# Three score blocks of a slice in one run, and a new timetable, in a graph-attention layer on one Trainium2 core

## The chip, the core and the metric

The kernel runs on one core of a Trainium2 chip. A core has TensorE (PE, matrix products, with the loading of its weights shown as PEld), VectorE (DVE), ScalarE (ACT), GpSimd (POOL) and SyncE (SP), each with its own instruction stream, and DMA queues that move data between the chip's main memory and the on-chip memory SBUF. PE writes to PSUM, a small memory that DVE and ACT read. The metric is device time in microseconds of one execution, as the median of several runs.

## What is computed

128 graphs of 128 nodes and 768 features, 12 heads of 64, everything in 32-bit floats. In short:

```python
h = maximum(layernorm(x), 0)
q, k, v = split_heads(h @ Wq + bq), split_heads(h @ Wk + bk), split_heads(h @ Wv + bv)
s = einsum('bhqd,bhkd->bhqk', q, k) / sqrt(64) + beta * adj
s = where(adj > 0, s, -9e15)
out = x + merge_heads(einsum('bhqk,bhkd->bhqd', softmax(s), v))
```

## The kernel before

**Groups and slices.** Four graphs make a group (G, 32 of them). For each group the projections come in three slices: `qk0` (Q and K of heads 0 to 5), `v`, and `qk1` (Q and K of heads 6 to 11). A slice is a product of 512 rows by 768 by 768. From group 1 on it is made in the manner of fast matrix multiplication: the 2x3 blocks of activations and 3x3 blocks of weights are combined so that 15 products (`PRODUCTS`) replace the 18 of the plain way, and each of them again takes 7 zones in place of 8. Group 0 goes the plain way (`plain_slice`), while the combined weights (T tiles, 448 KB each) are made and stored in main memory.

**A product** (L681, in `product`) is 7 zones of two 64-column halves, 28 instructions in the trace. Products with the same chain letter (a to d) add up in the same PSUM pair; after each, `evict` takes the running sum out into the home of each block of the result in which it is used. The first that a home receives opens it: before, for Q and K, three ACT operations (640 columns at L724, then twice 128 with the bias at L726); for V, DVE adds the bias to 256 columns (L711) and ACT copies the other 640 (L716). All later ones are DVE accumulations of 896 columns (L704). There are 4 PSUM pairs; a chain's next product has to wait until the evictions of the one before it have read the pair. When a block is complete, `decode` adds its zones (four POOL operations at L739 to L742 for Q and K, five at L750 to L754 for V); DECODE says when, and for a few blocks that DVE does it ("v").

**Attention.** A block `oc` (0 to 5) is a pair of heads for the group's four graphs. `scores` (L776, 32 instructions on 64x64 quarters) writes to a PSUM pair, `mask` (L789, DVE) adds the bias and frees the pair, `expo` (L798, ACT) takes the exponential, `attend` (L855, 32 instructions) multiplies by V, `drain` (ACT), `recip` (DVE), `divide` (eight ACT operations), `add` (DVE, L904) and `send` (SP) finish it. An attend is a generator: `turn()` emits 4 of its instructions after each zone of the products that follow. The three blocks of `qk0` are scored while the V slice runs, those of `qk1` while the next group's `qk0` runs. `to_hT` (L580, DVE) turns the activations of the next group, `inner` (POOL) and ten `sum_acts` (L585, DVE) combine them.

**The order** of every engine's stream is written out: `put(at, f)` puts an action on a heap of due times, and after each product `slice_z` runs what is due. A group is 45 slots long, one for each product: `qk0` has slots 0 to 14, `v` 15 to 29, `qk1` 30 to 44, and a time past 45 lies in the next group. TABLE has the due times of a group, FIRST, SECOND and LAST exceptions for the first and last groups, EVICT and DECODE the offsets of evictions and decodes from their product, ORDER the order of the products in a slice. Group 0's slices go by another mechanism (`then(n, f)`: lists of actions for each product, and `later`, `trailing`, `masking`).

**Transfers.** 10 of the 45 T tiles stay in SBUF (RESIDENT gives their positions in the sequence of 45). The others come through a ring of 6 buffers; `load_T` issues the next load (SP) right behind the product that frees a buffer.

## Time and profile before

| | |
|---|---|
| median of 3 runs | 2667.59 us (2667.44 to 2669.44) |
| span of the profiled execution | 2664.1 us |
| mean granted clock of PE | 0.998 |
| first product of group 1 begins at | 122.1 us |
| DMA: moved, mean rate | 736.65 MB, 277 GB/s |

The span goes from the first to the last instruction of the profiled execution; a time of that execution by the clock of the runs isn't given, and the median of the runs is 3.5 us longer than the span. The page gives each engine's busy time, the chain of work that ended last, and the costliest groups of instructions (line, engine, operation, output and inputs, count, busy time and mean ns of one, idle time before them and what ended it). The timeline merges like instructions and gives start, duration and count; a duration of merged PE rows reaches to the end of the last instruction, which overlaps with the next row.

### The profile page before, as it was taken

To read this page: it belongs to the slowest core of one execution; us is meant where nothing else is said; L and a number is where in the kernel's file an instruction comes from. 1 tells how busy PE (TensorE), PEld (TensorE's weight loads), DVE (VectorE), ACT (ScalarE), POOL (GpSimd) and SP (SyncE) were. 2 spreads that over 40 slices of the span, in tenths; PEclk is the share of its full clock that TensorE was granted. 3 is DMA by queue.
4 is the path that set the end of the run, shared out by engine and by line. 5 is a ranking of instruction groups with operands and counts; after the bars stand their busy time and mean duration, and the time that the engine had idled before them with its cause. 6 is when DMAs were issued, how large, how long until landed. Compare 5 with 4: busy or idle time off the path is not lost.

```text
span 2664.1 us, 121442 instructions
## 1 busy us (share of the span) xinstructions
PE 2644.1 (99%) x52041; PEld 2564.2 (96%) x52041; DVE 2165.8 (81%) x2702; ACT 1755.1 (66%) x4608; POOL 2097.8 (79%) x3043
## 2 busy tenths in 40 slices
PE   9999999999999999999999999999999999999998
PEld 8799999999999999999999999999999999999997
DVE  7878887878888788887788887888877888778876
ACT  2567766677666677666777666776667776667654
POOL 5877778877779777788777797777887777887774
PEclk9999999999999999999999999999999999999999
DMA  8899999998989999999999899999899898999885
GB/s 254 276 281 279 282 284 278 283 292 267 293 281 279 287 277 284 281 281 280 289 269 288 281 281 282 288 275 285 279 278 292 268 291 279 276 286 282 256 253 165
DMA packets 531572, 736.65 MB, mean 277 GB/s; under 512 B 106444, under 2 KB 371160, under 8 KB 531032
## 3 DMA queue, kind: packets, MB, share of 16 engines
q1 hardware_dynamic: 530384, 728.06, 88.5%
q8 instruction: 411, 6.73, 1.0%
q14 instruction: 129, 1.06, 0.1%
q10 hardware_dynamic: 648, 0.79, 0.1%
HBM read 662.22 MB, written 66.51 MB: 274 GB/s over the span
## 4 chain that ended last, share of the span: by engine, by line
PE 94%; DVE 1%; DMA 0%; issue 0%; ACT 0%; SPq 0%; DVEq 0%; ACTq 0%
PE pair L681 80%; PE pair L776 7%; PE pair L855 6%; PE pair L1048 1%; DVE home L704 0%; DMA x<-in_x_dram 0%; DMA T_qk<-kept_qk 0%; PE pair L926 0%; DVE e L789 0%; DVE prep_qk L403 0%; ACT e L836 0%; DVE res_qk L403 0%; PE pair L947 0%; DVE e L931 0%; ACT e L933 0%
## 5 line engine op out<-in xcount | busy, mean ns | idle before, releaser
L704 DVE TENSOR_TENSOR home<-home,pair 128x896 f32<-128x896 f32 x836 | 880.0, 1077 | 220.5 <-PE pair L681 179.8
L681 PE MATMUL pair<-sbig,T_qk 128*64 128x128 f32 x13020 | 827.6, 274 | 2.3 <-DVE home L704 1.2
L681 PEld LDWEIGHTS pair<-sbig,T_qk 128*64 128x64 f32 x13020 | 702.5, 137 | 19.9 <-issue 12.1
L739 POOL TENSOR_TENSOR home<-home 128x256 f32<-128x256 f32 x308 | 266.1, 864 | 320.0 <-DVE home L704 319.7
L681 PE MATMUL pair<-T_v,sbig 128*64 128x128 f32 x7812 | 457.8, 273 | 1.6 <-ACT home L716 0.6
L681 PE MATMUL pair<-A,T_qk 128*64 128x128 f32 x6944 | 445.6, 273 | 0.9 <-issue 0.9
L681 PEld LDWEIGHTS pair<-T_v,sbig 128*64 128x64 f32 x7812 | 430.7, 137 | 8.4 <-ACT e L836 4.8
L855 PE MATMUL pair<-v,e 128*64 128x65 f32 x6048 | 403.5, 221 | 0.0
L836 ACT ACTIVATE e<-e,sm 128x64 f32<-128x64 f32 x1512 | 381.7, 341 | 7.4 <-DVE sm L824 6.1
L681 PEld LDWEIGHTS pair<-A,T_qk 128*64 128x64 f32 x6944 | 384.6, 137 | 1.5 <-issue 1.5
L855 PEld LDWEIGHTS pair<-v,e 128*64 128x64 f32 x6048 | 362.2, 137 | 3.2
L724 ACT ACTIVATE home<-pair 128x640 f32<-128x640 f32 x340 | 240.6, 708 | 188.5 <-PE pair L681 187.2
L681 PE MATMUL pair<-sbig,res_qk 128*64 128x128 f32 x4340 | 312.3, 273 | 0.4
L742 POOL TENSOR_TENSOR home<-home 128x256 f32<-128x256 f32 x308 | 269.7, 876 | 24.1
L885 ACT ACTIVATE sm<-pair,tiny 128x8 f32<-128x8 f32 x189 | 50.8, 269 | 329.5 <-PE pair L855 329.5
L789 DVE SCALAR_TENSOR_TENSOR e<-pair,biasT 128x1024 f32<-128x1024 f32 x189 | 229.4, 1214 | 34.1 <-PE pair L776 33.0
L740 POOL TENSOR_TENSOR home<-home 128x256 f32<-128x256 f32 x308 | 228.2, 741 | 24.1
L681 PEld LDWEIGHTS pair<-sbig,res_qk 128*64 128x64 f32 x4340 | 238.0, 137 | 1.4 <-DVE home L704 1.3
L560 ACT ACTIVATE x<-x,block 128x192 f32<-128x192 f32 x480 | 222.6, 540 | 0.0
L726 ACT ACTIVATE home<-pair,bqk 128x128 f32<-128x128 f32 x680 | 214.3, 377 | 0.0
L798 ACT ACTIVATE e<-e 128x1024 f32<-128x1024 f32 x189 | 196.1, 1055 | 21.8 <-DVE e L789 14.0
L741 POOL TENSOR_TENSOR home<-home 128x128 f32<-128x128 f32 x308 | 175.6, 570 | 24.2
(208 smaller groups left out, 4401.6 us busy)
## 6 DMA issues: line engine op xcount, KB each, us to landing
T_qk<-kept_qk SPq DMA_DIRECT2D x713, 448.0 KB
T_v<-kept_v SPq DMA_DIRECT2D x372, 448.0 KB
xo<-in_x_dram SPq DMA_DIRECT2D x190, 256.0 KB
out_dram<-xo SPq DMA_DIRECT2D x189, 256.0 KB
x<-in_x_dram SPq DMA_DIRECT2D x248, 192.0 KB
sbig<-in_x_dram SPq DMA_DIRECT2D x116, 384.0 KB
kept_qk<-prep_qk SPq DMA_DIRECT2D x23, 448.0 KB
adj<-in_adj_dram SPq DMA_DIRECT2D x128, 64.0 KB
```

The lines of the kernel that those rows point to most:

```text
L560: nc.scalar.activation(t, t, AF.Relu, bias=shift[G, n], scale=rstd[G, n])
L681: nc.tensor.matmul(p[q:q + HD, at, :], lhs[:, q:q + HD], rhs, start=(first and at % 4 == 0), stop=True, skip_group_check=True)
L704: nc.vector.tensor_tensor(t, t, p[:, 0:7], op)
L724: nc.scalar.activation(t[:, 0:5], p[:, 0:5], AF.Copy, scale=float(sign))
L726: nc.scalar.activation(t[:, at], p[:, at], AF.Identity, bias=bqk[:, of, oc:oc + 1], scale=float(sign))
L739: e.tensor_tensor(t[:, 1:4:2], t[:, 1:4:2], twice(5), ALU.add)
L740: e.tensor_tensor(t[:, 2:5:2], t[:, 2:5:2], twice(1), ALU.add)
L742: e.tensor_tensor(t[:, 0:7:6], t[:, 0:7:6], twice(2), ALU.add)
L789: nc.vector.scalar_tensor_tensor(e[:, :, at], ps[:, :, at], SCORE_CAP * ISCALE, bias[:, :, at], op0=ALU.min, op1=ALU.add)
L798: nc.scalar.activation(e, e, AF.Exp, scale=1.0 / ISCALE)
L836: nc.scalar.activation(o[:, r, b, 0:HD], pa[:, r, b, 0:HD], AF.Copy, scale=t[:, 1, r, b:b + 1])
L855: nc.tensor.matmul(pa[q:q + HD, 2 * g + i, :], k[:, q:q + HD], vt[G, "v", r, h // 4][:, 4 * g + h % 4, :], start=True, stop=True, skip_gro ...
```

## The change

- **Score runs.** In TABLE, the three `scores` entries of each Q/K slice get due times that fall in one slot, with no other PE work due between them (before: two in one slot, the third some slots later). The blocks of a run come in another sequence (1, 0, 2 and 0, 2, 1 of the slice's three).
- **Product orders.** One ORDER for all groups (the last group's `qk1` keeps its own); the first slice begins 4, 1, 8, 5, which completes chain d before the scores.
- **Openings.** OPEN, empty before, names products whose opening goes another way: 2 is all on DVE, 1 splits off the last 384 columns (Q, K) to DVE. With the new orders and offsets, 2 takes effect in a middle group for two openings of `qk0` (both uses of product 4) and three of `v` (both of product 4, and product 5). `bqk` grows to 8 columns, the first five zero, so that one DVE operation adds the bias to 896 columns.
- **Attends.** Blocks in WHOLE (2, 3, 5) are emitted in one piece.
- **Decodes.** All new offsets. In a middle group DVE decodes V block (1, 1) and Q/K block (0, 2) of `qk1`; before, only block (0, 0) of `qk1`.
- **Timetable.** TABLE, EVICT, DECODE and LAST anew, EARLY for group 0's actions in place of its lists, OVER for single entries of the first groups. RESIDENT names other positions.
- `needs` and `did` only check the order while the program is built; they issue nothing.

```diff
-ORDER = {"qk0": (1, 0, 5, 2, 10, 3, 6, 7, 13, 11, 9, 4, 14, 12, 8), "v": (1, 0, 5, 2, 10, 3, 6, 7, 13, 11, 4, 9, 14, 8, 12), "qk1": (4, 1, 0, 8, 2, 5, 3, 6, 7, 10, 9, 13, 11, 12, 14)}
+ORDER = {'qk0': (4, 1, 8, 5, 0, 3, 2, 10, 7, 6, 11, 9, 13, 14, 12), 'v': (4, 1, 8, 5, 3, 10, 0, 7, 2, 13, 6, 11, 9, 14, 12), 'qk1': (4, 0, 3, 8, 2, 1, 7, 6, 5, 9, 11, 10, 12, 14, 13)}
-RESIDENT = (10, 12, 16, 21, 29, 33, 36, 39, 41, 42)
+RESIDENT = (0, 5, 14, 16, 22, 24, 27, 31, 38, 39)
 TABLE = (
...
-    (5.399, 'sum', 'S5'), (8.41, 'sum', 'S14'), (9.857, 'sum', 'S11'), (17.129, 'scores', 0, 2),
-    (17.594, 'mask', 2), (18.011, 'exp', 2), (17.884, 'scores', 0, 1), (20.163, 'mask', 1),
-    (23.187, 'exp', 1), (23.44, 'scores', 0, 0), (24.691, 'mask', 0), (26.808, 'xo', 2),
...
-    (47.396, 'scores', 1, 2), (47.912, 'mask', 5), (47.949, 'scores', 1, 0), (49.895, 'add', 0),
-    (49.151, 'mask', 3), (51.424, 'send', 0), (50.757, 'exp', 5), (51.214, 'scores', 1, 1),
...
+    (8.583782, 'sum', 'S11'), (9.005184, 'sum', 'S5'), (9.963287, 'sum', 'S14'), (18.715354, 'scores', 0, 1),
+    (18.71757, 'mask', 1), (18.718354, 'scores', 0, 0), (18.721354, 'scores', 0, 2), (19.858615, 'mask', 2),
+    (19.938663, 'exp', 2), (26.447577, 'exp', 1), (27.850478, 'mask', 0), (35.49811, 'xo', 2),
...
+    (45.127516, 'attend', 0), (45.60572, 'divide', 1), (48.381413, 'drain', 0), (48.750402, 'add', 1),
+    (48.785602, 'recip', 0), (48.985172, 'scores', 1, 0), (48.988172, 'scores', 1, 2), (48.991022, 'mask', 3),
+    (48.991172, 'scores', 1, 1), (49.260051, 'mask', 5), (51.074388, 'divide', 0), (51.320856, 'send', 1),
...
+    (0, 'drain', 4): 61.5908, (2, 'norm', 3, 2, 4): 66.1614, (2, 'sum', 'S1'): 81.7354, (0, 'drain', 5): 60.3658,
...
+    (0, 'exp', 4): 58.1173, (1, 'xo', 3): 102.7651, (0, 'scores', 1, 0): 48.8393, (0, 'recip', 3): 56.1085,
...
+WHOLE = (2, 3, 5)
 OPEN = {
+    ('qk0', 0): 2, ('qk0', 3): 2, ('qk0', 4): 2, ('qk0', 7): 1, ('qk0', 8): 2, ('qk0', 10): 2,
+    ('qk0', 11): 1, ('qk0', 12): 2, ('qk0', 13): 1, ('qk1', 8): 2, ('qk1', 9): 1, ('qk1', 10): 1,
+    ('qk1', 11): 2, ('qk1', 13): 1, ('v', 0): 1, ('v', 4): 2, ('v', 5): 2, ('v', 6): 2,
+    ('v', 7): 1, ('v', 9): 2, ('v', 12): 1,
 }
...
                 bias = bv_b[:, j * 2 * P:(j + 1) * 2 * P].rearrange("p (i n) -> p i n", i=2)
                 nc.vector.tensor_tensor(t[:, 5:7], bias, p[:, 5:7], op)
-                if split:
+                if split == 2:
+                    nc.vector.tensor_scalar(t[:, 0:5], p[:, 0:5], float(sign), None, op0=ALU.mult)
+                elif split:
...
-                if split:
+                if split == 2:
+                    nc.vector.tensor_tensor(t, bqk[:, 0:7, oc:oc + 1].to_broadcast([P, 7, P]), p[:, 0:7], op)
+                elif split:
...
     def attend(G, oc, behind=None):
-        between.append(attend_steps(G, oc, behind))
+        steps = attend_steps(G, oc, behind)
+        if (G or oc > 2) and oc in WHOLE:
+            for _ in steps:
+                pass
+        else:
+            between.append(steps)
...
+    def run_until(at):
+        while events and events[0][0] < at:
+            _, _, f, args = heapq.heappop(events)
+            f(*args)
...
     for G in range(NG):
...
+        for n, (at, name, *args) in enumerate(TABLE):
+            if placed(G, at, name, args):
+                put(OVER.get((G - NG if G == NG - 1 else G, name, *args), max(45 * G + at, 45 + 0.001 * n)), actions[name], G, *args)
```

The exceptions in OVER that concern scores are: group 0, `scores` 1, 2 at 46.7153 and 1, 0 at 48.8393; group 1, 0, 0 at 63.8665, 1, 0 at 93.9684 and 1, 1 at 94.5242; group 2, 0, 0 at 108.7881 and 0, 2 at 108.7766.

## The prediction

> **What bounds the kernel now.** I read the page's busy table and its chain that ended last first, then TensorE's (PE's) waits, then its timeline.

> ```profile
> span 2664.1 us, 121442 instructions
> ...
> PE 2644.1 (99%) x52041; PEld 2564.2 (96%) x52041; DVE 2165.8 (81%) x2702; ACT 1755.1 (66%) x4608; POOL 2097.8 (79%) x3043
> ...
> PE 94%; DVE 1%; DMA 0%; issue 0%; ACT 0%; SPq 0%; DVEq 0%; ACTq 0%
> PE pair L681 80%; PE pair L776 7%; PE pair L855 6%; PE pair L1048 1%; DVE home L704 0%; DMA x<-in_x_dram 0%; DMA T_qk<-kept_qk 0%; PE pair L926 0%; DVE e L789 0%; DVE prep_qk L403 0%; ACT e L836 0%; DVE res_qk L403 0%; PE pair L947 0%; DVE e L931 0%; ACT e L933 0%
> ```

> The end is set by PE: 94% of the chain is PE following PE. L681 are the products, L776 the scores, L855 the attends. The waits of PE say how little another engine holds it up:

> ```profile
> PE pair L1369 <- DVE over L970: 3.6, 1, 3.6
> PE pair L681 <- issue: 2.4, 6, 1.1
> PE pair L681 <- DVE home L704: 2.2, 2, 1.2
> ```

> Columns: total us, times, longest. In 2664 us the products wait 2.2 us for an eviction. So an edit on DVE, ACT or POOL can gain almost nothing here, only lose; a gain must come out of PE's own stream. There, one group repeats; the chain in order of time has the same piece at

> ```profile
> 919.46 4.80 PE pair L681 x88
> ...
> 1000.51 4.80 PE pair L681 x88
> ```

> that is, every 81.05 us. One slice of such a group, on PE:

> ```profile
> 1048.19 1.70 PE L681 MATMUL pair<-res_v,sbig 128*64 128x128 f32 x28
> 1049.72 1.70 PE L681 MATMUL pair<-T_v,sbig 128*64 128x128 f32 x28
> 1051.34 1.98 PE L776 MATMUL pair<-home 64*64 64x128 f32 x64
> 1053.25 4.81 PE L681 MATMUL pair<-T_v,sbig 128*64 128x128 f32 x84
> 1057.89 1.70 PE L681 MATMUL pair<-res_v,A 128*64 128x128 f32 x28
> 1059.41 3.23 PE L681 MATMUL pair<-T_v,sbig 128*64 128x128 f32 x56
> 1062.57 1.10 PE L776 MATMUL pair<-home 64*64 64x128 f32 x32
> 1063.61 3.28 PE L681 MATMUL pair<-T_v,A 128*64 128x128 f32 x56
> 1066.71 3.23 PE L681 MATMUL pair<-T_v,sbig 128*64 128x128 f32 x56
> ```

> Columns: start, duration, instructions; only differences of starts count, since durations overlap. A product (28 instructions) takes 1049.72 - 1048.19 = 1.53 us. From 1049.72 to 1057.89 lie four products and two score blocks (x64): 8.17 - 6.12 = 2.05 us for the two. From 1059.41 to 1066.71 lie four products and one block (x32): 7.30 - 6.12 = 1.18 us. So a further block in a run costs 2.05 - 1.18 = **0.87 us**, and a run costs **0.31 us** beside its blocks, whatever its length. The shapes show where it lies: the scores use 64x64 quarters of the array, the products 128x64 halves, and PE loses time on the way in (1051.34 is 0.09 after 1049.72 + 1.53) and out.

> ```profile
> 1004.93 0.39 PE L681 MATMUL pair<-sbig,T_qk 128*64 128x128 f32 x4
> 1005.15 0.40 PE L855 MATMUL pair<-v,e 128*64 128x65 f32 x8
> ...
> 1007.39 1.70 PE L681 MATMUL pair<-sbig,res_qk 128*64 128x128 f32 x28
> ```

> An attend is woven into one product; that product takes 2.46 us, so the attend 0.93. Check: 45 x 1.53 + 6 x 0.93 + 2 x (2.05 + 1.18) = 80.9 of the 81.05. The group is accounted for by PE alone.

> **The change, part by part.** *Score runs.* Before: each of the 61 Q/K slices scored in groups 1 to 31 (31 first ones, 30 second ones; the last is cut in halves) has a run of two and one of one, 122 runs; group 0 adds 6: 128. After: one run of three a slice, where the three entries fall in one slot with no other PE work between them (18.715 to 18.721 and 48.985 to 48.991, slot 18 and slot 3). Exceptions are read from OVER: group 0's second slice has two runs (46.7; 48.8 and 48.99), group 1's second two (93.97 and 93.99; 94.52). That gives 3 + 2 + 1 + 2 + 30 + 29 = 67. 61 runs go: 61 x 0.31 = **19.0 us less**. A run of three isn't in the trace; I take 1.18 + 2 x 0.87 = 2.92, the step from one to two repeated. Bounds: nothing, if a third block were as dear as a run of its own (1.18), and these 19.0: 0.87 is 32 instructions at half of a product's pace (1.53 / 28 = 0.0546), two at once, and a block has no reason to go below that.

> *Attends whole.* WHOLE emits blocks 2, 3 and 5 (93 in all) in one piece instead of woven in. The end of the kernel has such a piece:

> ```profile
> 2644.17 1.10 PE L947 MATMUL pair<-v,e 128*64 128x65 f32 x32
> 2645.10 0.39 PE L681 MATMUL pair<-sbig,T_qk 128*64 128x128 f32 x4
> ```

> 32 instructions of the same shape in 0.93 us: as much as woven. I take 0. [...]

> *Openings, decodes, DVE.* OPEN moves two Q/K openings from ACT to DVE in the first slice (one 128x896 operation each, instead of three on ACT) and the 640-column part of three V openings; one V decode goes from POOL to DVE. ACT (66%) and POOL (79%) only gain. The rows for DVE:

> ```profile
> L704 DVE TENSOR_TENSOR home<-home,pair 128x896 f32<-128x896 f32 x836 | 880.0, 1077 | 220.5 <-PE pair L681 179.8 <-POOL A L590 36.7 <-ACT sbig L521 2.1
> L789 DVE SCALAR_TENSOR_TENSOR e<-pair,biasT 128x1024 f32<-128x1024 f32 x189 | 229.4, 1214 | 34.1 <-PE pair L776 33.0
> L904 DVE TENSOR_TENSOR xo<-xo,e 128x512 f32<-128x512 f32 x186 | 161.8, 870 | 0.1
> L580 DVE STREAM_TRANSPOSE A<-x 128x512 f32<-128x512 f32 x186 | 129.2, 696 | 0.1
> L585 DVE TENSOR_TENSOR sbig<-sbig,A 128x896 f32<-128x896 f32 x93 | 118.5, 1274 | 1.0
> ...
> L742 DVE TENSOR_TENSOR home<-home 128x256 f32<-128x256 f32 x32 | 28.3, 883 | 1.1
> L740 DVE TENSOR_TENSOR home<-home 128x256 f32<-128x256 f32 x32 | 26.4, 825 | 1.1
> ...
> L741 DVE TENSOR_TENSOR home<-home 128x128 f32<-128x128 f32 x32 | 21.8, 681 | 1.1
> L739 DVE TENSOR_TENSOR home<-home 128x256 f32<-128x256 f32 x32 | 20.6, 644 | 0.0
> ```

> Operations overlap by some 0.08 us: four back to back take 4.08, not 4 x 1.08:

> ```profile
> 1067.00 4.08 DVE L704 TENSOR_TENSOR home<-home,pair 128x896 f32<-128x896 f32 x4 [0.51 <-PE pair L681]
> ```

> Added for a group: 2 x 1.0, 3 x 0.75 (5/7 of a row of L704, which also reads PSUM), and a V decode, five operations of 128 or 256 columns like those of L739 to L742: nothing to 3.8, I take 3.0. That is 7.2 us on an engine with 81% of 81 us, so near 90%. The first slice is the full one. By the new due times it holds, on DVE, 11 accumulations and 2 openings (13.0), 3 masks (3 x 1.13), 5 activation sums (5 x 1.19), a Q/K decode (2.7), 2 adds (1.6) and 3 turns (1.9): **28.5 us**, against PE's 15 x 1.53 + 2 x 0.93 + 2.92 = **27.7**. Before, that slice had

> ```profile
> 1000.50:1029.50 29.00, 29.00 (x590) 28.42 (x586) 25.10 (x28) 19.64 (x60) 25.85 (x31) 1.00 0.89 277
> ```

> (PE, PEld, DVE, ACT, POOL busy): DVE 25.1 of 29.0. The overflow of 0.8 us runs into the V slice, where DVE has some 21 us of work in 27.7. So it needn't stop PE, but the places are tight. Product 8 follows product 4 on the same PSUM pair after one product only and must wait for both evictions of 4, 2.1 us on DVE; the attend due in slot 45.1 lies woven into that product (1.53 + 0.93 = 2.46), which leaves 0.4 us for both hand-overs. The product behind a run of three takes the pair that the first mask frees: the mask has two blocks, 1.74 us, for its 1.21. Bounds: 0, and the whole overflow, 0.8 us a group. I take 0.1 a group (a fourth of one such margin), 30 x 0.1 = **3 us more**.

> *Product orders, residents, DMAs.* The work stays: 45 products a group at 1.53, ten tiles kept, so 35 loads of 448 KB a group as before. The longest stretch of the sequence without a kept tile falls from 12 products (positions 43 to 9) to 8 (6 to 13). SP's issues (inputs, sends, loads of T) are the same in number; each T load still stands behind its product, whose pace sets it. 0.

> *Start and end.* Group 0's actions get due times of their own, group 1 other offsets, the last group's V slice another order. The two wait rows of L681 (2.4 + 2.2) hold what can go; bounds -4.6 and, as much again added, +4.6. Group 1's first slice has one of the two DVE waits (1.2) and a new order: I take **-1**.

> Sum for the profiled execution: span 2664.1 - 19.0 + 3.0 - 1.0 = 2647.1. The median, 2667.6, lies 3.5 above the span; I take that as unchanged: **2650.6 us**.

> **The rivals.** *DVE becomes the bound in the first slice.* For it: 28.5 against 27.7. Against: the V slice gives it back, and PSUM holds four pairs. Price: 0.8 x 30 = 24 instead of 3: 2671.6 if all of it stops PE, 2659.6 if half; within 0.2% for the most part.

> *POOL's decodes come late for three blocks at once* (the slower side). A run of two needed four of six decoded tiles; the run of three needs all six, and the last block had five more slots before.

> ```profile
> L739 POOL TENSOR_TENSOR home<-home 128x256 f32<-128x256 f32 x308 | 266.1, 864 | 320.0 <-DVE home L704 319.7
> ...
> L742 POOL TENSOR_TENSOR home<-home 128x256 f32<-128x256 f32 x308 | 269.7, 876 | 24.1
> ...
> L740 POOL TENSOR_TENSOR home<-home 128x256 f32<-128x256 f32 x308 | 228.2, 741 | 24.1
> ...
> L741 POOL TENSOR_TENSOR home<-home 128x128 f32<-128x128 f32 x308 | 175.6, 570 | 24.2
> ```

> One decode is 3.05 us on POOL. For the V slice's run, four stand in a row behind the eviction of product 9: 12.2 us. On PE, from the end of product 9 to the third block lie products 13, 14, 12, then 4, 1, 8, 5 (7 x 1.53), two attends (1.86) and two blocks (1.83): 14.4. Less about 1.1 for that eviction, some 1 us remains. If DVE's lag eats this and one operation more (0.75), PE waits 0.75 in each of 61 runs: 46 us, 2696. It decides from 0.31 a run.

> *Whole attends wait for weights.* At a load per 54.6 ns, the product's own pace (1.53 / 28), 32 take 1.75: 0.82 x 93 = 76 us, 2727. The row of L947 speaks against. [...]

> *The runs aren't joined* (PE work slips between): 2669.6, the sum without the 19. Against: the due times.

> **How the numbers follow.** My forecast, 2644 to 2660: 0.74. A larger gain, all waits of the start gone (below 2644): 0.03. DVE's bound: 0.12, a quarter of it still faster. Runs not joined: 0.02. POOL's decodes: 0.08. Whole attends: 0.01. The range 2643 to 2666 leaves out POOL, the attends, the unjoined runs, about half of DVE's case and part of the larger gain, 0.19. 0.2% is 5.3 us, about what a measurement of this kernel can tell from no change: faster 0.74 + 0.03 + 0.03 = 0.80, within 0.11, slower 0.09.

> **What would show it.** In the changed profile: score rows of x96 on PE, 2.92 us of cost by the same difference of starts; the period of a group at 80.4; attends of x32 in 0.93; DVE near 90%; PE's waits for L704 small. Rows "scores <- POOL home" would show the POOL rival, products waiting for DVE by whole microseconds a group the DVE one. I am wrong if the period stays at 81 or above.

## The result, and the profile after

| | before | after |
|---|---|---|
| median | 2668.52 us (4 runs, 2667.44 to 2670.2) | 2770.25 us (4 runs, 2758.72 to 2776.61) |
| span of the profiled execution | 2664.1 us | 2767.5 us |
| mean granted clock of PE | 0.998 | 0.996 |
| first product of group 1 | 122.1 us | 123.3 us |

The ratio is 1.0374 (95% interval 1.0349 to 1.0398): 102 us slower, where 17 us faster was forecast. In the changed kernel the products are at L796, the scores at L901, the attends at L990. The page of the changed kernel, its busy table and its chain:

```profile
span 2767.5 us, 121305 instructions
...
PE 2657.5 (96%) x52041; PEld 2584.2 (93%) x52041; DVE 2344.5 (85%) x3018; ACT 1640.2 (59%) x4327; POOL 1901.2 (69%) x2883
...
q1 hardware_dynamic: 529856, 727.80, 90.8%
q8 instruction: 411, 6.73, 1.0%
...
PE 92%; issue 4%; DMA 2%; DVE 2%; SPq 0%; ACT 0%; POOL 0%; ACTq 0%; DVEq 0%; POOLq 0%
```

PE has the same 52041 matmuls, and the chain still runs on PE, but 4% of it is now "issue", which was 0%: time in which an engine waits for nothing that the profile shows. PE's waits in the changed kernel (total us, times, longest):

```profile
PE pair L796 <- issue: 47.3, 41, 3.1
PE pair L901 <- issue: 32.1, 30, 3.1
PE pair L990 <- issue: 7.8, 10, 1.7
PE pair L1494 <- DVE over L1107: 3.6, 1, 3.6
PE pair L559 <- DVE st L547: 2.4, 1, 2.4
PE pair L796 <- DMA T_v<-kept_v: 2.4, 1, 2.4
```

Over all rows of this view, PE's waits for other engines and for data sum to 17.7 us, against 13.1 before. Its waits for "issue" went from 2.6 us (7 times) to 87.2 us (81 times). The windows view of the same stretch in both kernels (us, then busy us and instructions of PE, PEld, DVE, ACT, POOL, then clock, DMA share, GB/s), first before:

```profile
300.00:2600.00 2300.00, 2297.42 (x46566) 2249.61 (x46564) 1879.96 (x2234) 1561.80 (x4102) 1848.13 (x2653) 1.00 0.91 280
```

and after:

```profile
300.00:2600.00 2300.00, 2215.83 (x44632) 2175.63 (x44628) 1963.13 (x2417) 1410.17 (x3717) 1595.24 (x2408) 1.00 0.94 270
```

PE stood 2.6 us there before and 84.2 us after, and got through 4% fewer matmuls.

**What "issue" is here.** The timeline of PE in the changed kernel, around one stop:

```profile
672.35 1.70 PE L796 MATMUL pair<-T_v,A 128*64 128x128 f32 x28
673.88 1.70 PE L796 MATMUL pair<-T_v,sbig 128*64 128x128 f32 x28
675.50 2.88 PE L901 MATMUL pair<-home 64*64 64x128 f32 x96
678.31 2.84 PE L796 MATMUL pair<-T_v,sbig 128*64 128x128 f32 x48
683.60 2.19 PE L796 MATMUL pair<-T_v,sbig 128*64 128x128 f32 x36 [2.45 <-issue]
```

PE stops in the middle of a product, after 20 of its 28 instructions, where it can wait for no tile. The row "q8 instruction" above has 411 packets of 16 KB, and from the start of one to the start of the next PE began 256.1 instructions in the mean, in either kernel (matmuls and weight loads counted together, with the few others of PE). The stop lies, by the count below, at one and the same place of every 256; I call it a block boundary. The DMA view of 681.0 to 682.2 us has one of them:

```profile
q1 hardware_dynamic: 94, 0.30, 85.7%
q8 instruction: 1, 0.02, 5.6%
```

and the same view from 676 to 681 has none, only data, 103.9% of the time of the engines by this view:

```profile
q1 hardware_dynamic: 716, 1.34, 103.9%
```

By the trace's record this packet, from here on a **refill**, ran from 681.08 to 682.16, and PE went on at 683.60. I numbered PE's instructions and looked at every gap: 101 lie at the same place, within three instructions of 194 past a multiple of 256, and sum to **107.4 us** above the usual pitch. Before: 10 such gaps, 3.1 us. (The sum depends on the usual pitch that is taken off: with the median step from one matmul's start to the next, the same 101 gaps give 115.0 us, and the 10 before 3.9.) All other gaps went from 15.3 to 20.2 us. So the span comes apart as 2664.1 - 19.0 (score runs, below) + 104.3 (these stops) + 4.9 (other gaps) + 5.3 (an estimate: 0.2% for the mean granted clock, 0.996 where it was 0.998) = 2759.6, against 2767.5; 8 us I could not place, about what the choice of the pitch makes.

A refill can be followed in three pieces: from PE passing the instruction 165 past a multiple of 256 (a fixed mark of mine; between 300 and 2500 us each refill of both kernels began 12 instructions behind it or later) to its start, the **wait**; its own duration, 1.06 us before and 1.12 after; and from its end to PE going on, 1.47 us at the stops (middle eight tenths 1.33 to 1.64). From the mark to the place of the stops behind the next multiple of 256 (193 past it) lie 284 instructions. How long PE takes for them is the **cover**: a slice with dense short instructions has a short one (5.5 us at slot 3 of the changed kernel, 7.7 at slot 24). PE stopped where wait + 1.1 + 1.5 was more than the cover: between 300 and 2500 us this sum, taken refill by refill, names all 83 of the gaps over 0.3 us at this place in the changed kernel and all 7 in the one before, and 20 and 8 refills more, late by 0.33 and 0.22 us at most. Means by the slot in which PE passes the mark, in us, and the stops that followed between 300 and 2500 us, worked out from the trace:

| slot | wait before | cover before | wait after | cover after | stops after |
|---|---|---|---|---|---|
| 3 | 2.6 | 6.9 | 2.8 | 5.5 | 0.8 |
| 6 (after: 5) | 3.8 | 6.3 | 3.1 | 7.3 | 0.0 |
| 15, 16 | 3.5, 3.7 | 6.2, 6.3 | 4.6, 4.7 | 6.3, 6.2 | 27.0 |
| 18 | 2.6 | 7.6 | 5.5 | 6.1 | 29.4 |
| 24, 25 | 2.0, 1.2 | 7.6 | 2.2, 1.7 | 7.7 | 0.0 |
| 37, 41 | 1.7, 1.8 | 6.7, 7.1 | 4.6, 5.8 | 6.8, 7.3 | 23.9 |

Two things changed: the waits grew (mean 2.47 to 3.49 us, longest 5.0 to 7.3), most at slots 15 to 18 and 37 to 1; and where scores lie closer together the cover shrank, since score instructions passed in about half the time (96 in 2.88 us, against 28 in 1.53). Put through the same rule one refill after the other, the changed kernel's waits and covers give 101 us; its covers with waits of before, drawn slot by slot, 9 us; its waits with covers of before 80 us. So, by this working, the refills' lateness is the larger part, and before there was hardly any room: at slot 6, 3.8 + 1.1 + 1.5 is 6.4 for a cover of 6.3.

### The profile page after: what moved, and what is told of

Same layout as the page of the kernel before. It is cut to its first block, busy times and chain, and to the rows that moved or that the text cites. A ratio compares the mean times of both kernels' runs of the same rounds, so it can differ in the third digit from the quotient of the medians.

```text
span 2767.5 us, 121305 instructions
## 1 busy us (share of the span) xinstructions
PE 2657.5 (96%) x52041; PEld 2584.2 (93%) x52041; DVE 2344.5 (85%) x3018; ACT 1640.2 (59%) x4327; POOL 1901.2 (69%) x2883
## 4 chain that ended last, share of the span: by engine, by line
PE 92%; issue 4%; DMA 2%; DVE 2%; SPq 0%; ACT 0%; POOL 0%; ACTq 0%; DVEq 0%; POOLq 0%
PE pair L796 76%; PE pair L901 6%; PE pair L990 6%; PE pair L1185 3%; DMA xo<-in_x_dram 1%; DVE home L820 1%; DMA sbig<-in_L_gnn_Wk_dram 0%; PE pair L1403 0%; DMA sbig<-in_x_dram 0%; DMA out_dram<-xo 0%; PE pair L1190 0%; DVE sbig L690 0%; SPq L412 0%; DMA T_v<-kept_v 0%; DVE e L915 0%
## 5 line engine op out<-in xcount | busy, mean ns | idle before, releaser
L796 PE MATMUL pair<-sbig,T_qk 128*64 128x128 f32 x13888 | 866.9, 273 | 9.2 <-issue 7.2
L796 PEld LDWEIGHTS pair<-sbig,T_qk 128*64 128x64 f32 x13888 | 782.2, 137 | 15.8 <-issue 12.8
L796 PE MATMUL pair<-A,T_qk 128*64 128x128 f32 x6944 | 427.0, 273 | 2.5 <-DVE sbig L839 1.6
L796 PEld LDWEIGHTS pair<-A,T_qk 128*64 128x64 f32 x6944 | 386.6, 137 | 3.9 <-issue 1.9
L796 PE MATMUL pair<-T_v,sbig 128*64 128x128 f32 x5208 | 320.1, 276 | 33.3 <-issue 30.5
L796 PEld LDWEIGHTS pair<-T_v,sbig 128*64 128x64 f32 x5208 | 294.6, 138 | 43.0 <-issue 41.1
L990 PE MATMUL pair<-v,e 128*64 128x65 f32 x6048 | 323.4, 221 | 8.7 <-issue 7.8
L990 PEld LDWEIGHTS pair<-v,e 128*64 128x64 f32 x6048 | 300.1, 137 | 16.1 <-issue 12.0
L796 PE MATMUL pair<-T_v,A 128*64 128x128 f32 x4340 | 260.4, 273 | 0.1
L796 PE MATMUL pair<-res_v,sbig 128*64 128x128 f32 x3472 | 239.4, 273 | 1.7 <-issue 1.7
L796 PEld LDWEIGHTS pair<-T_v,A 128*64 128x64 f32 x4340 | 239.3, 137 | 1.5 <-ACT home L835 0.4
L655 ACT ACTIVATE x<-x,block 128x192 f32<-128x192 f32 x480 | 226.1, 540 | 6.4 <-DMA T_v<-kept_v 3.6
L901 PE MATMUL pair<-home 64*64 64x128 f32 x5312 | 182.9, 274 | 26.4 <-issue 26.3
L796 PE MATMUL pair<-sbig,res_qk 128*64 128x128 f32 x3472 | 207.3, 273 | 0.5 <-issue 0.5
```

Of the source, the lines that this page charges most:

```text
L655: nc.scalar.activation(t, t, AF.Relu, bias=shift[G, n], scale=rstd[G, n])
L796: nc.tensor.matmul(p[q:q + HD, at, :], lhs[:, q:q + HD], rhs, start=(first and at % 4 == 0), stop=True, skip_group_check=True)
L901: nc.tensor.matmul(ps[k:k + HD, i, g * N:(g + 1) * N], keys[r, k:k + HD], queries[r], start=True, stop=True)
L990: nc.tensor.matmul(pa[q:q + HD, 2 * g + i, :], k[:, q:q + HD], vt[G, "v", r, h // 4][:, 4 * g + h % 4, :], start=True, stop=True, skip_gro ...
```

## The experiments

The theories: **data**, refills come late because of the data transfers' timetable (RESIDENT, input loads, SP's order); **density**, PE's instructions lie too densely (runs of three, whole attends), whatever the data do. In the texts that were on record ahead of the runs, the letters change: up to e7_light_before and in e11_split1, A is both together, B the data alone and C density alone; in e8_x_times, e9_resident, e12_all_dma and e13_res2, B is the data, with B1 for the input loads and B2 for the T loads; in e4_before_whole and from e14_res3 on, A is the data. In e17_x_late a "trigger" is PE passing the mark. Runs without a ratio beside them are single executions, and the four of the changed kernel lie up to 18 us apart; so they are read by their stops first.

**Density.** e1_woven and e3_split and e5_woven_split change the changed kernel; e11_split1 too; e4_before_whole changes the kernel before.

```diff
-WHOLE = (2, 3, 5)                      # e1, e5 (drains 4 and 5 a slot later)
+WHOLE = ()
-(18.721354, 'scores', 0, 2)            # e3, e5 (with its mask and exp)
+(20.72, 'scores', 0, 2)
-(48.991172, 'scores', 1, 1)
+(51.2, 'scores', 1, 1)
-(18.721354, 'scores', 0, 2)            # e11
+(19.75, 'scores', 0, 2)
-(48.991172, 'scores', 1, 1)
+(49.9, 'scores', 1, 1)
```

> The changed kernel with WHOLE = (): all attends woven into products again, the drains of blocks 4 and 5 one slot later so that they stand behind their attends. Score runs stay joined. Theory A (PE's instruction blocks of 256 arrive late because the joined score runs and whole attends use them up too fast AND because the refill stands behind data transfers): some of the 107 us of stops at block boundaries goes, time 2700 to 2745 us. Rival B (only the backlog of data transfers of the new timetable makes the refill late; how dense PE's instructions are doesn't matter): 2760 to 2775, as the changed kernel. Rival C (only density matters): like A here.

2780.8 us, stops 95.3 us: the time didn't fall and the stops did by 12 us only, so whole attends don't make most of the loss.

> The changed kernel with the third score block of each run taken two slots later (18.72 to 20.72 and 48.99 to 51.2, groups 1 and 2 partly as they were), so runs of two and one again; attends stay whole. About 57 runs more: +18 us in every theory. A: the stops in slots 18 to 21 (70 of 107 us) fall by half or more, sum 2720 to 2755. B: nothing but the runs, 2780 to 2795. C: as A or lower.

2826.3 us, stops 85.4, but other gaps 78.4. The two largest of PE's waits are

```profile
PE pair L797 <- DVE e L916: 37.6, 28, 1.3
PE pair L902 <- issue: 37.1, 32, 2.7
```

The first is a wait for a mask that this edit itself makes late. The stops fell by 22 us, where theory A asked for 35 at slots 18 to 21 alone; the time, outside every forecast because of that mask, says nothing.

> The edits of the two runs before together: attends woven, score runs of two and one; what stays of the change are product orders, evictions, openings, decodes, residents and timetable. A: PE's instructions are about as dense as in the kernel before, stops below 25 us, time 2675 to 2700 us (two and one costs 18 more than three). B: 2780 to 2795. C: 2665 to 2685.

2859.0 us, stops 90.3, other gaps 99.5, with the same mask's wait (38.9 us). With attends woven and runs of two and one, as in the kernel before, the stops stay.

> The changed kernel with the third block of each score run one product later (18.72 to 19.75 and 48.99 to 49.9; mask and exponential stay where they are, so DVE isn't held up as in e3_split). The runs cost 18 us more in every theory. Density of PE's instructions matters (A, C): the stops in slots 18 to 21 fall from 70 to below 40, total 2735 to 2765. It doesn't (B): stops as before, 2780 to 2795.

2782.8 us, stops 97.7: the forecast for density not mattering. These edits are weaker tests of density than I took them for: the 284 instructions of a cover reach over four or five products, and an attend, woven or whole, or a third block one product later, lies within the same cover. e11_split1 raised it at slot 18 only from 6.1 to 6.5 us. A stronger one, for the attends, emits all 186 of them in one piece on the data timetable of before:

```diff
-        while between and next(between[0], None) is None:
-            between.popleft()
+        while between:
+            for _ in between.popleft():
+                pass
```

> Edit: the kernel before, with every attend emitted in one piece behind its product instead of four instructions after each zone. Theory A (data transfers): the data timetable is that of before, refills stay in time, stops at block boundaries stay under 8 us, and the time is within 5 us of before. Rival (dense pieces of short instructions use up a block of 256 too fast, whatever the data do): 186 dense pieces give stops of 20 us and more, 2685 or above.

2666.6 us against 2664.7, stops 1.8 us. Here, with the refills in time, whole attends cost nothing that can be told from the spread of the kernel before (2662.75 to 2668.9). A run of three on that timetable was not tried.

**Lighter data.** In both kernels each streamed T tile brings four of its seven zones, and the products use these four again for the rest, so numbers are others.

```diff
-            nc.sync.dma_start(t, kept[sl, n])
+            nc.sync.dma_start(t[:, 0:4], kept[sl, n][:, 0:4])
-            lhs, rhs = a[:, LEFT[z]], b[:, RIGHT[z]]
+            lhs, rhs = a[:, LEFT[z]], b[:, RIGHT[z] % 4 if streamed else RIGHT[z]]
```

> The changed kernel with loads of the streamed T tiles cut to 4 of their 7 zones; products of streamed tiles use zones 0 to 3 in place of 4 to 6, so the numbers computed are others, with the same instructions on PE. Data traffic falls by about 35 x 0.19 MB of 22 MB a group, some 30%. A and B: the refill no longer stands behind a backlog, stops at block boundaries fall below 10 us, time 2645 to 2665 us. C (density alone, a fixed delay of the refill): stops stay near 100 us, time above 2740.

20130.8 us: the changed numbers set off the kernel's second way of computing the layer, `general`, which runs behind the first. As a time it tells nothing; between 122 and 2650 us PE stood 21.1 us, 16.4 of them for "issue". So once more without `general`, and the same for the kernel before:

> The changed kernel with the streamed T tiles loaded to 4 of 7 zones (products of streamed tiles use zones 0 to 3 in place of 4 to 6, so other numbers come out) and without the second path `general`, which those numbers would set off. If the late refills come from data traffic (A or B) and the rest of the prediction holds: no stops at block boundaries, group period 80.4 to 80.7, time 2645 to 2660 us. C (density alone): above 2740.

> The same two edits in the kernel before (other numbers come out here too): 2660 to 2668 us, a few us less than before at most, since it has 3 us of stops. The difference to the run with the changed kernel is what the change does without late refills; the prediction's terms (19.0 less in score runs, 3 more of waits) say 12 to 20 us less for the changed kernel.

2669.1 and 2659.8 us, with 195 and 196 GB/s between 300 and 2600 us in place of 270 and 280. The first is above its forecast of 2645 to 2660. Stops fell to 23.6 us in it, 22.9 of them at slot 19, and to none in the second. The wait of a refill fell to 1.7 us in the mean, but stayed at 4.6 and 4.0 at slots 15 and 16, just ahead of the run of three:

```profile
PE pair L898 <- issue: 19.4, 16, 2.1
PE pair L1491 <- DVE over L1104: 3.2, 1, 3.2
```

Without its stops the light changed kernel would take 2669.1 - 23.6 = 2645.5, 14 us less than the light one of before. Its groups without a stop show the same: each took 80.3 to 80.7 us, where 80.4 was forecast, and the light kernel before needed 81.0 in most. The gain that the prediction counted is there, under the loss.

**The timetable of the data, part by part.** Each into the changed kernel, but e10_res_before into the kernel before.

```diff
-    (-55.883236, 'load_x', 0, (0,)), (-53.825602, 'load_x', 0, (3,))     # e8, e12, e13
+    (-53.424, 'load_x', 0, (0,)), (-50.853, 'load_x', 0, (1,))
...
-RESIDENT = (0, 5, 14, 16, 22, 24, 27, 31, 38, 39)
+RESIDENT = (10, 12, 16, 21, 29, 33, 36, 39, 41, 42)                     # e9, e12
+RESIDENT = (12, 14, 15, 16, 17, 36, 38, 40, 41, 43)                     # e13
-RESIDENT = (10, 12, 16, 21, 29, 33, 36, 39, 41, 42)                     # e10
+RESIDENT = (0, 5, 14, 16, 22, 24, 27, 31, 38, 39)
-(57.954175, 'xo', 3)                                                    # e12
+(53.5, 'xo', 3)
```

> The changed kernel with the due times of the eight quarter loads of x from the kernel before (slots 11.9 to 14.3 in place of 12.4 to 16.4, and 36.6 to 40.6 in place of 34.1 to 38.7). Theory B1 (the backlog at slots 13 to 18 and 36 to 44 is made by x and xo loads falling together): stops fall by a third or more, time below 2740. B2 (the backlog is made by the T loads, whose gaps the residents set): 2755 to 2780.

2742.6 us, stops 69.1: the stops fell by over a third, as B1 has it, the time to just above its bound.

> The changed kernel with the kernel before's RESIDENT (positions 10, 12, 16, 21, 29, 33, 36, 39, 41, 42). B2: the T loads fall in other slots, none issued behind the products at 36, 39, 41, 42, so the stops in slots 41 to 1 go and the time falls below 2740, or new ones come elsewhere and it moves by over 20 us either way. B1: 2755 to 2785.

2712.3 us, stops 52.2: the places of the residents alone are worth 58 us. The waits of PE:

```profile
PE pair L796 <- issue: 25.2, 23, 2.4
PE pair L901 <- issue: 19.1, 16, 2.3
```

> The kernel before with one part of the change alone: RESIDENT of the changed kernel. If the residents' positions by themselves bring the late refills: over 20 us of stops at block boundaries, 2685 us or more. If they do so only with the rest of the new timetable: stops below 8 us, 2664 to 2675.

2689.9 us, 22 more than before, stops 18.2 (13.8 at slot 18, right behind the run of two). The same ten positions thus cost time in either kernel, without a single run of three:

```profile
PE pair L681 <- issue: 10.9, 14, 3.2
PE pair L776 <- issue: 3.8, 7, 1.3
```

> The changed kernel with RESIDENT and the x load times of the kernel before, and xo 3 loaded 4.5 slots earlier (53.5). B, the parts adding up (28 us and 58 us less, found alone): stops below 35 us, 2680 to 2700. If both act on the same stops: 2700 to 2715.

2709.1 us, stops 52.0, all but a few at slots 19 to 21. The gains of the two edits before don't add up: with the input loads moved as well it is no better than e9_resident. The waits of refills whose mark PE passed at slots 16 and 19 were still 4.4 and 4.7 us.

> The changed kernel with the x load times of the kernel before and residents at positions 12, 14, 15, 16, 17, 36, 38, 40, 41, 43, so that hardly a T load is issued while the x and xo loads of slots 12 to 17 and 36 to 43 run. B: the refill's wait at slots 15 to 20 and 37 to 0 (4 to 6 us) falls to that of the kernel before (2 to 4), stops below 25 us, 2660 to 2690. Against it: 18 products in a row without a kept tile ask for T at 448 KB a product, so PE may wait for T loads from slot 25 on: then over 2700.

2731.7 us, stops 25.3, but other gaps 70.5. With 18 products in a row that have no kept tile (positions 18 to 35), the ring runs dry there, as was feared:

```profile
PE pair L796 <- DMA T_v<-kept_v: 20.9, 24, 1.9
PE pair L796 <- DMA T_qk<-kept_qk: 19.3, 24, 4.8
```

**Which transfers?** Three guesses at a simple rule, none of which held:

```diff
-RESIDENT = (0, 5, 14, 16, 22, 24, 27, 31, 38, 39)                       # e14, e15
+RESIDENT = (5, 10, 11, 13, 20, 21, 29, 32, 34, 38)
-(58.948939, 'xo', 5)                                                    # e15
+(61.0, 'xo', 5)
-(-30.448024, 'load_x', 1, (1,))                                         # e15
+(-31.1, 'load_x', 1, (1,))
-(-47.512641, 'turn_in')                                                 # e15
+(-46.6, 'turn_in')
...
-        src = x[...].rearrange("g (b i) (a f) -> a i (g b) f", i=SQ, a=NB)      # e16, from group 3 on
+        src = x[...].rearrange("g (h i b) f -> (g h) i (b f)", h=2, i=SQ)
```

> Edit: the changed kernel with RESIDENT = (5, 10, 11, 13, 20, 21, 29, 32, 34, 38), nothing else. These positions were chosen by an account of the data that is outstanding at each slot: what SP's due times and the products issue, less 0.30 MB a us. In that account the changed kernel peaks at 2.2 MB at slot 14 and 1.6 MB at slot 38, the kernel with the residents of before at 1.9 and 1.6; this one nowhere passes 1.0. Theory A (PE's instruction refills come late because they queue behind data that is outstanding, and the places of T loads among the input loads decide it): the stops of PE at its block boundaries fall from 107 us to under 30, the mean wait of a refill from 3.5 us to about 2.5, and the time to 2655-2690. Theory B (it is the work itself in the new order, or the input and output transfers, and residents are only a part): it stays with the run that had the residents of before, 2700-2715, or above.

2718.8 us (ratio 1.0185, 1.0162 to 1.0207), stops 68.3, waits of 5.1 and 4.8 at slots 15 and 18 though my account had levelled the bytes. The sum of bytes outstanding, as I counted it, isn't the rule. (The 0.30 MB a us in it is an estimate: 280 GB/s at a DMA share of 0.91 before and 270 at 0.94 after, in the windows above, make 0.31 and 0.29 at a full share.)

> Edit: as e14_res3, and three SP entries moved: xo 5 from 58.9 to 61.0 (so that it no longer waits for the output that leaves its buffer, with T loads queued behind it), load_x 1 part 1 from -30.4 to -31.1, turn_in from -47.5 to -46.6. Theory A with the detail that SP's queue being held up bunches T loads: SP's waits of 47.7 us (L886, for the output) and 66.2 us (L635) shrink by more than half, and the time is 5-15 us below e14_res3. If only the residents matter: the same as e14_res3 within 4 us.

2730.9 us (1.0238, 1.0221 to 1.0255), stops 78.2. SP's wait at L635 fell as meant, 60.8 us in e14_res3 to 28.5, and the time rose: this pause of SP isn't what counts.

> Edit: the changed kernel, where load_x from group 3 on fetches each part (192 KB into 32 partitions) as runs of whole rows, 6144 B a partition, in place of eight pieces of 768 B. Same bytes, same issues, same due times; the activations of these groups are at other places than the reference has them. Theory A1 (the 768-B pieces hold the refills back: over all refills of the changed kernel the wait goes with 6.7 us per MB of such pieces outstanding, with 0.6 per MB of the 3584-B ones): refill waits at slots 15 to 20 and 37 to 1 fall from 4-6 us to 3.5 or less, stops from 107 us to under 50, the time to 2715 or less. Theory A2 (only how much is outstanding, whatever its pieces): 2750-2780 as before.

2761.0 us, stops 100.1, waits as in the changed kernel (5.6 at slot 18). (The activations come to lie elsewhere, so its numbers are others.) The size of the pieces isn't it; what else makes the long waits go with these loads, this run doesn't show.

**Their place.** With the residents of before, the four input loads of rows 1 go behind the score run instead of ahead of it, and the norms and the turn that need them a few slots later:

```diff
-(-32.569114, 'load_x', 1, (0,))
+(-24.6, 'load_x', 1, (0,))             # e17; -25.5 in e18
...
-(-20.7282, 'turn', 'A11')
+(-18.6, 'turn', 'A11')                 # e17; -16.4 in e18
```

> Edit: the changed kernel with the residents of before (2712 us so) and the four load_x parts of rows 1 moved from slots 12.4-16.4 to 20.4-22.5, behind the score run of slot 18, their norms and one turn 2 to 3 slots later. Numbers and work as in the reference. Theory A1 or A2 (these loads are what delays the refills that the run of slot 18 needs): the stops of triggers at slots 15 to 18, about three quarters of that run's 52 us, fall under 12 us, and the time to 2665-2690. If T loads alone hold the refills: 2700-2715. If the later norms hold up the turns: waits of DVE and PE for ACT appear, 2720 and more.

2990.3 us (1.1209, 1.118 to 1.1238), stops 12.9. In 28 groups DVE stood at the turn, in its order ahead of evictions, for these loads, and PE for DVE. DVE's timeline, with PE's row behind it in the next fence:

```profile
1004.25 1.09 DVE L820 TENSOR_TENSOR home<-home,pair 128x896 f32<-128x896 f32 x1 [0.47 <-PE pair L796]
1013.93 0.71 DVE L678 STREAM_TRANSPOSE A<-x 128x512 f32<-128x512 f32 x1 [8.60 <-ACT x L655]
```

(L655 is the norm on ACT, which itself waited 7.96 us for the load of x.)

```profile
1015.67 3.26 PE L796 MATMUL pair<-T_v,sbig 128*64 128x128 f32 x28 [8.49 <-DVE home L820]
```

These waits of PE sum to 252.7 us, and its granted clock was 0.948, against 0.994 in e9_resident.

> Edit: as e17_x_late (residents of before, input loads of rows 1 behind the score run of slot 18), but the four parts go out at slots 19.5 to 20.1, ahead of the row load and the adj loads that held the last part up to slot 25.5 there, and the turn that stood 8.6 us on DVE waiting for it comes at slot 28.6 (from 26.4), its inner at 29.8. Numbers and work as in the reference. Theory A (the place of these loads decides the refills that the run of slot 18 needs; the 278 us of e17_x_late are DVE held up behind this turn): stops at block boundaries stay under 20 us, as in e17_x_late (12.9 us), PE's waits for DVE fall from 253 us to under 15, and the time is 2655-2680, against 2712 with the residents of before alone. Rival (the refills were in time there only because PE stood 8 to 10 us in each group): stops come back to 40 us and more, 2695 or above.

2739.1 us (1.0271, 1.0257 to 1.0285), stops 34.1, between its two forecasts, with a time as long as the rival's. But by place it is clear. Waits of refills in us and stops by the slots where PE stood:

| | wait at 16 | at 18 | at 24 | at 41 | stops, slots 19 to 21 | stops, slots 41 to 5 |
|---|---|---|---|---|---|---|
| e9_resident (loads ahead of the run) | 4.0 | 4.6 | 2.0 | 4.4 | 45.1 | 6.1 |
| e18_x_late2 (loads behind it) | 2.7 | 2.0 | 4.0 | 5.6 | 3.3 | 30.0 |

The long waits went along with the loads, from slot 18 to slot 24, where the cover of 7.6 us was long enough (4.0 + 2.6 = 6.6), and the stops at the run of three, with the run and its density unchanged, all but vanished, though PE no longer stood there as in e17_x_late. What was saved came back in two places: stops at slots 41 to 5, whose loads weren't touched, and T tiles that now land behind the moved loads, in each group at slot 28:

```profile
PE pair L796 <- DMA T_v<-kept_v: 38.3, 27, 2.4
PE pair L796 <- issue: 16.0, 18, 2.0
PE pair L901 <- issue: 5.8, 10, 1.1
```

No version of the changed kernel that keeps the numbers beat the kernel before.

## Why the prediction was wrong, point by point

- **What bounds the kernel: PE's own stream.** True, but read too narrowly. The row "PE pair L681 <- issue: 2.4, 6, 1.1" was in front of me, and I put it with the start and the end. Five of its six waits, 1.3 us, lie at block boundaries, far from the start: refills that were already only just in time. (The sixth, 1.1 us at 126.4 us, is no boundary.) PE waited for almost nothing in 2664 us, and I took that for room. A group took 84.8 us in the mean, against 81.4 before: the sign of being wrong that the prediction named.
- **Score runs, 19.0 us less.** The mechanism and the size hold. The changed kernel's timeline has, at slot 3 of a group,

```profile
471.93 1.75 PE L796 MATMUL pair<-A,T_qk 128*64 128x128 f32 x28
473.51 1.70 PE L796 MATMUL pair<-sbig,T_qk 128*64 128x128 f32 x28
475.14 2.85 PE L901 MATMUL pair<-home 64*64 64x128 f32 x96
477.92 1.75 PE L796 MATMUL pair<-sbig,T_qk 128*64 128x128 f32 x28
```

  477.92 - 473.51 - 1.53 = 2.88 for a run of three; 2.92 was forecast. The two light kernels show 14 us net once the stops are taken off, start and rest included.
- **Whole attends, 0.** Right: 32 instructions in 0.94 us by

```profile
368.35 1.10 PE L990 MATMUL pair<-v,e 128*64 128x65 f32 x32
369.29 3.23 PE L796 MATMUL pair<-sbig,res_qk 128*64 128x128 f32 x56
```

  and e4_before_whole.
- **Openings and decodes, 3 us more.** Too dear, if anything. DVE's work grew by 178.7 us, where 30 x 7.2 = 216 were counted, yet PE's longest row for it within the groups is 1.6 us once (L839).
- **Product orders, residents, DMAs, 0.** This is the step that failed: "each T load still stands behind its product, whose pace sets it. 0." In its place stand 104 us of late refills. I asked whether data would come late for PE's products, and only one T load did (2.4 us). I did not ask what else the DMA carries. PE's instructions came by it as well (411 packets on q8, one for 256), and a refill's wait had room for 2.8 to 5 us in these slots (covers of 5.4 to 7.6 less 2.6). Moving the ten kept tiles alone cost 22 us in the kernel before and 58 us in the changed one; the input loads' times, by themselves, 28 (the two together 61, so they don't add). The score runs' term has a part in it too: it counted a denser run as time saved alone, and a denser run also shortened the cover (slot 18: 7.6 to 6.1 us), which by the sum with the waits of before makes stops of 9 us.
- **Start and end, -1.** 1.2 us later at the first product of group 1; small either way.
- **The rivals.** None came true. POOL's decodes cost 1.2 us once (L796 <- POOL sbig), DVE didn't bind, the runs were joined, attends didn't wait for weights. Missing was a rival on PE's supply of instructions, for which the price could have been worked out: a mean wait of 2.47 us and covers of 6.2 to 7.6 stand in the trace of before, and a fourth of the 411 refills late by 1 us is 100 us.

What stays open is why a refill began late beside some transfers and not beside others. Their places made a difference: the wait at slot 18 fell from 4.6 to 2.0 us with the input loads behind it (e18_x_late2), and the stops of the kernel before rose from 3.1 to 18.2 us with other kept tiles (e10_res_before). The sum of bytes outstanding (e14_res3, stops 68.3), the pieces' size (e16_x_big, 100.1) and SP's pauses (e15_res3_spread, 78.2) don't explain it by themselves. The trace doesn't say which of the 16 engines carried a packet, so what else the engine of a refill carried can't be followed. Nor was the share of density settled by a run of its own: that it is the smaller part rests on the sum with exchanged waits and covers, and on e18_x_late2 and e4_before_whole. With residents and input loads put back (e12_all_dma) 52 us of stops remained, and which of the other differences makes them isn't shown. Stops at slots 41 to 5 were not tried alone.

## What to carry to other kernels

Where PE is busy nearly all the time and the DMA as well (99% of the span and a share of 0.91 before), look at how late the instruction refills come before moving any transfer: gaps called "issue" that recur at one place of the count of instructions were late refills here (101, 107.4 us), and what counted was the wait against the time that PE needed for the 284 instructions up to that place (at slot 18 a wait of 5.5 us, with 1.1 and 1.5 behind it, against 6.1). A dense run of short instructions (here the quarter-array scores, 96 in 2.88 us) right behind a bunch of input loads is a place to look at first: 56.4 us of the stops between 300 and 2500 us followed marks at slots 15 to 18, and with the loads behind the run the stops at slots 19 to 21 were 3.3 us in place of 45.1 (e18_x_late2, e9_resident), while the time rose from 2712.3 to 2739.1. In this case the timetable of transfers was part of PE's schedule though PE waited for a single T load (2.4 us) in the changed kernel: in e10_res_before the positions of the kept tiles alone cost 22 us.
